# A convolution and mixture-of-experts kernel: the W stage's result kept as [output channel, w]

## The chip, the cores and the metric

The kernel runs on one core of one Trainium2 chip, in one launch. The metric is device microseconds for one execution. The names of the engines are those of the profile: PE is TensorE's matmul, PEld its load of the stationary operand, DVE VectorE, ACT ScalarE, POOL GpSimd, SP SyncE.

## The reference

Everything is fp32. Layer 0 is a convolution made of butterfly transforms along both image axes, added to its input after a group norm; layer 1 is an attention over the batch axis and a top-2 mixture of 8 experts, both on the tokens. Cut to what matters:

```python
# x: (32, 128, 64, 64); H = W = 64
def _kop2d(x, weight, kd1, kd2, k11, k12, k21, k22):
    xc, wc = x.astype(complex64), weight.astype(complex64)      # weight (128, 128, 3, 3)
    x_f = tensor_product(xc, _c(k11), _c(k12), False)           # butterflies along H, then along W
    w_f = tensor_product(wc, _c(kd1), _c(kd2), False) * math.sqrt(H * W)
    prod = jnp.einsum('bihw,oihw->bohw', x_f, w_f)
    return jnp.real(tensor_product(prod, _c(k21), _c(k22), True))

x = x + _kop2d(_gn(x), ...)                       # group norm over 32 groups of 4 channels
t = _to_tokens(x)                                 # (32, 4096, 128)
t = t + _L1_attn_ref(_ln_t(t), Wk, bk, Wv, bv)    # softmax((K^T V) / sqrt(32)) applied to the tokens
t = t + _L1_ffn_ref(_ln_t(t), ...)                # router, top 2 of 8 experts, weighted sum
x = _from_tokens(t, x)
```

## The kernel before

The butterflies are multiplied out at the start into dense matrices, and as the weight has only 3 x 3 taps the convolution becomes a sum over its rows p and columns q of three matrix products: over input channels, along w, along h. The 32 images are worked one after another, and each image's convolution runs in three rounds, one for each p. A round has three stages:

- `mix` (matmuls at L284): 16 groups g of two matmuls. The normalised image is the stationary operand, 128 pixels at a time, `wmix` (384 columns) the moving one. Four copies a group take the result out of PSUM into `y` [(q, w), channel, h].
- `along_w`, the W stage (matmuls at L304 and L312): 8 groups. The stationary operand is a contiguous piece of `y` with two channels, the moving one `ra` (128 columns) or `rb` (256). Each group fills two PSUM banks. Four copies a group take the result out into `u`, whose partitions are (real or imaginary, h). Each copy moves 64 partitions x 512 elements: 4 x 2 runs of 64 values of w, one run for each output channel.
- `along_h`, the H stage (matmuls at L334): 4 groups of 16 matmuls. Each takes all 128 output channels at one w from `u` as the stationary operand, and `lt[:, p, :]` with 64 columns as the moving one. DVE adds the group to the image (L338).

The trace holds two LDWEIGHTS and two MATMUL records for every `matmul` of the code: 64 matmuls of an H stage are 128 records.

The order is written by hand through generators: the H stage of a round is issued after the mix of the next round, so mix, H stage of the round before, W stage follow each other on TensorE, 96 times. All conv stages share two PSUM buffers of two banks (tag `cv`), and `y` and `u` are single buffers. An image's tail, which is the transposition to tokens, the attention and the experts (`tail`, L387 to L567), is cut into pieces, and a scheduler at the end of the kernel lays them between the pieces of the next image's convolution by estimated costs. The copies out of PSUM go through `evacuate`, which gives every fourth to DVE (L249) and the others to ACT (L251); copies of `y`, `u` and of the tail share this turn and these two lines. The program puts a wait between two copies of one group where one is on DVE and the other on ACT, so the four of a group run one after another.

On each engine instructions run in program order. An engine that waits for a copy holds up what is behind it.

## Time and profile before

| | |
|---|---|
| median of the runs | 12064.9 us (12059.3 to 12070.5, two runs) |
| profiled execution, span | 12065.3 us |
| PE busy | 10224.3 us, 85% |
| PEld busy | 7555.0 us, 63% |
| DVE busy | 6990.2 us, 58% |
| ACT busy | 6791.9 us, 56% |
| matmuls of the H stage (L334) | 12288 records, 1424.5 us busy |
| copies of u, ACT and DVE | 2304 and 768, 1036 and 1039 ns each |
| HBM traffic | 11 GB/s over the span |

Busy time is an average over stages that are held by different engines. The chain of waits says what set the end: it is followed back from the last instruction to what released it each time, and its shares are shares of the span. In the groups of instructions each line has engine, line of the kernel, operation, output and inputs, shapes and count; behind the first bar the busy time in all and the mean duration of one, behind the second the idle time before them and what ended most of it. TensorE's durations overlap in its pipe, so its pace is read from busy time and count, or from rows of consecutive matmuls. PEclk is the granted share of TensorE's clock.

### The profile page before, as it was taken

Reading aid. Unit: us, or ns where it says so; the run is one execution under the profiler, and the core shown is the slowest. Engines: PE = TensorE matmul, PEld = TensorE weight load, DVE = VectorE, ACT = ScalarE, POOL = GpSimd, SP = SyncE. Lnnn points to the kernel's source line nnn. Section 1 sums busy time; section 2 is a strip of 40 time slices with the busy share of each in tenths; the row PEclk is TensorE's granted clock in tenths of the full one; section 3 lists DMA queues with packets and bytes.
Section 4 is the critical chain, followed back from the end, with each engine's and each line's share of the span. In section 5 each row is a group of like instructions: output and inputs, shape, how many; then the busy total and the mean of one; then the engine's idle time right before and its main releaser. Section 6 shows DMA issues by size and latency. Waiting matters only on the chain.

```text
span 12065.3 us, 140418 instructions
## 1 busy us (share of the span) xinstructions
PE 10224.3 (85%) x53944; PEld 7555.0 (63%) x53944; DVE 6990.2 (58%) x17483; ACT 6791.9 (56%) x8609; POOL 694.6 (6%) x378
## 2 busy tenths in 40 slices
PE   6888888888888888888888888888888888888888
PEld 4666666666666566666666666665666666565665
DVE  4456655556555565555665555655556555566556
ACT  5655555565555655556555555556565555656552
POOL 0000000000000000000000000000000000000000
PEclk9999999999999999999999999999999999999998
DMA  0000000000000000000000000000000000000000
GB/s 27 9 13 8 15 12 13 12 15 8 13 12 13 14 8 13 13 13 13 8 14 12 13 13 12 11 12 13 12 15 8 13 12 13 14 8 14 12 6 13
DMA packets 44636, 146.90 MB, mean 12 GB/s; under 512 B 5186, under 2 KB 6596, under 8 KB 39876
## 3 DMA queue, kind: packets, MB, share of 16 engines
q1 hardware_dynamic: 42096, 137.19, 3.1%
q8 instruction: 432, 7.08, 0.2%
q14 instruction: 232, 1.90, 0.1%
q10 hardware_dynamic: 1876, 0.73, 0.0%
HBM read 70.79 MB, written 67.11 MB: 11 GB/s over the span
## 4 chain that ended last, share of the span: by engine, by line
PE 54%; ACT 31%; DVE 9%; issue 3%; POOL 3%; DMA 0%; POOLq 0%; ACTq 0%; DVEq 0%
ACT y L251 22%; PE ph L334 12%; PE pw L304 10%; PE pw L312 10%; PE pe L539 8%; DVE y L249 5%; PE pm L284 5%; ACT u L251 5%; POOL rs L383 3%; ACT at L462 3%; PE pl L488 3%; PE pg L414 2%; DVE u L249 1%; PE po L554 1%; PE po L555 1%
## 5 line engine op out<-in xcount | busy, mean ns | idle before, releaser
L251 ACT COPY u<-pw 64x512 f32<-64x512 f32 x2304 | 2386.4, 1036 | 3421.3 <-PE pw L312 2445.5
L251 ACT COPY y<-pm 64x384 f32<-64x384 f32 x4608 | 3728.4, 809 | 959.4 <-DVE y L249 526.6
L284 PE MATMUL pm<-wmix,xn 128*128 128x384 f32 x6144 | 2611.7, 550 | 1176.3 <-ACT y L251 708.9
L544 DVE SCALAR_TENSOR_TENSOR t<-pe,oh,t 128x128 f32<-128x128 f32 x8192 | 2771.4, 349 | 396.7 <-PE pe L539 108.1
L284 PEld LDWEIGHTS pm<-wmix,xn 128*128 128x128 f32 x6144 | 1137.2, 205 | 2437.7 <-ACT y L251 1310.1
L304 PEld LDWEIGHTS pw<-ra,y 128*128 128x128 f32 x12288 | 1845.6, 192 | 372.3 <-issue 185.1
L539 PE MATMUL pe<-ew_sb,xT 128*128 128x512 f32 x4096 | 1956.0, 595 | 44.2 <-DVE t L544 43.4
L249 DVE COPY y<-pm 64x384 f32<-64x384 f32 x1536 | 1234.6, 804 | 1234.3 <-ACT y L251 1033.0
L304 PE MATMUL pw<-ra,y 128*128 128x128 f32 x12288 | 1906.3, 277 | 10.1 <-DVE u L249 6.8
L312 PE MATMUL pw<-rb,y 128*128 128x256 f32 x6144 | 1853.7, 384 | 0.0
L334 PEld LDWEIGHTS ph<-lt,u 128*128 128x128 f32 x12288 | 1421.9, 195 | 128.7 <-ACT y L251 69.8
L249 DVE COPY u<-pw 64x512 f32<-64x512 f32 x768 | 797.6, 1039 | 1209.0 <-ACT u L251 1206.7
L334 PE MATMUL ph<-lt,u 128*128 128x64 f32 x12288 | 1424.5, 278 | 25.6 <-ACT y L251 17.2
L539 PEld LDWEIGHTS pe<-ew_sb,xT 128*128 128x128 f32 x4096 | 757.4, 190 | 676.3 <-issue 402.9
L312 PEld LDWEIGHTS pw<-rb,y 128*128 128x128 f32 x6144 | 941.1, 194 | 4.2 <-issue 0.5
L338 DVE TENSOR_TENSOR x<-ph,x 128x1024 f32<-128x1024 f32 x384 | 470.3, 1225 | 755.6 <-PE ph L334 754.7
L368 DVE BATCH_NORM_STATS2 bs<-t 128x6 f32<-128x128 f32 x2048 | 427.0, 279 | 468.8 <-POOL t L466 468.8
L383 POOL TENSOR_TENSOR rs<-m,mhalf 128x32 f32<-128x32 f32 x64 | 347.8, 5435 | 4528.2 <-DVE m L382 4528.2
L414 PE MATMUL pg<-xg 128*128 128x129 f32 x2048 | 295.0, 300 | 201.0 <-DVE xg L409 201.0
L483 PE MATMUL px<-ident,xn 128*128 128x128 f32 x1024 | 252.5, 371 | 206.1 <-DVE xn L479 206.1
L466 POOL TENSOR_TENSOR t<-t,at 128x512 f32<-128x512 f32 x256 | 324.5, 1267 | 1672.1 <-ACT at L462 1647.9
L414 PEld LDWEIGHTS pg<-xg 128*128 128x128 f32 x2048 | 283.2, 215 | 210.3 <-DVE xg L409 194.2
(132 smaller groups left out, 5560.8 us busy)
## 6 DMA issues: line engine op xcount, KB each, us to landing
x<-in_x_dram SPq DMA_DIRECT2D x32, 2048.0 KB
out_dram<-so SPq DMA_DIRECT2D x256, 256.0 KB
tws<-in_tw_dram SPq DMA_DIRECT2D x6, 384.0 KB
wmix<-in_conv_w_dram SPq DMA_DIRECT2D x1, 576.0 KB
ew_sb<-in_expert_w_dram ACTq DMA_DIRECT2D x1, 512.0 KB
eb_sb<-in_expert_b_dram ACTq DMA_DIRECT2D x16, 4.0 KB
wk_sb<-in_wkT_dram ACTq DMA_DIRECT2D x1, 64.0 KB
wv_sb<-in_wvT_dram ACTq DMA_DIRECT2D x1, 64.0 KB
```

Of the source, the lines that this page charges most:

```text
L249: nc.vector.tensor_copy(dst, src)
L251: nc.scalar.copy(dst, src)
L284: nc.tensor.matmul(ps[:, k, 0:384], xn[:, r : r + P], wmix[:, p, :], start=True, stop=True)
L304: nc.tensor.matmul(ps[:, bank, c0 + ab * P : c0 + (ab + 1) * P], yf[:, o * n : (o + 2) * n], ra, start=(k % 2 == 0 and ab == 0), stop=False,)
L312: nc.tensor.matmul(ps[:, bank, c0 : c0 + 256], yf[:, o * n : (o + 2) * n], rb.rearrange("w a m -> w (a m)"), start=False, stop=(k % 2 == 1),)
L334: nc.tensor.matmul(pf[:, k * n : (k + 1) * n], u[:, 16 * g + k, :], lt[:, p, :], start=True, stop=True)
L338: nc.vector.tensor_tensor(acc, pf.rearrange("o (w h) -> o h w", h=n), acc, ALU.add)
L368: nc.vector.bn_stats(bs[:, t].rearrange("p a s -> p (a s)"), src[:, t, :])
L383: nc.gpsimd.tensor_tensor(rstd, var, mhalf, ALU.pow)
L414: nc.tensor.matmul(pg[:, 0 : P + 1], xt[:, k, 0:P], xt[:, k, :], start=(i == 0), stop=(i == NT - 1))
L539: nc.tensor.matmul(ps, xT[:, i, :], ew_sb[:, 4 * half : 4 * half + 4, :].rearrange("d e c -> d (e c)"), start=True, stop=True,)
L544: nc.vector.scalar_tensor_tensor(t[:, i, :], ps[:, k * P : (k + 1) * P], gates[:, i, 4 * half + k : 4 * half + k + 1], t[:, i, :], ALU.mul ...
```

## The change

`u` is allocated as [partition, output channel, w] in place of [partition, w, output channel]. The copies of the W stage, which read the same 64-element runs of PSUM as before, then write each run to 64 consecutive elements, where they wrote elements 128 apart. The H stage's stationary operand, all output channels at one w, was 128 consecutive elements and is now 128 elements that lie 64 apart (256 bytes). Comments are also taken out of the file; they are left out of this diff.

```diff
     def along_w(b, p, y, u):
         yf = y.rearrange("w o h -> w (o h)")
-        uv = u.rearrange("h w (ab j r) -> h j ab r w", ab=2, r=2)
+        uv = u.rearrange("h (ab j r) w -> h j ab r w", ab=2, r=2)
...
     def along_h(b, p, u, xt):
...
                 nc.tensor.matmul(
-                    pf[:, k * n : (k + 1) * n], u[:, 16 * g + k, :], lt[:, p, :], start=True, stop=True
+                    pf[:, k * n : (k + 1) * n], u[:, :, 16 * g + k], lt[:, p, :], start=True, stop=True
                 )
...
     def conv():
...
-                u = yp.tile([P, n, P], F32, tag="u", name=f"u{b}_{p}")
+                u = yp.tile([P, P, n], F32, tag="u", name=f"u{b}_{p}")
```

## The prediction

> **What bounds the kernel now.** I read the page's first and fourth parts, then the groups with their shapes, then the chain of waits and the stretches around two H stages.

> ```profile
> span 12065.3 us, 140418 instructions
> PE 10224.3 (85%) x53944; PEld 7555.0 (63%) x53944; DVE 6990.2 (58%) x17483; ACT 6791.9 (56%) x8609; POOL 694.6 (6%) x378
> ...
> PE 54%; ACT 31%; DVE 9%; issue 3%; POOL 3%; DMA 0%; POOLq 0%; ACTq 0%; DVEq 0%
> ACT y L251 22%; PE ph L334 12%; PE pw L304 10%; PE pw L312 10%; PE pe L539 8%; DVE y L249 5%; PE pm L284 5%; ACT u L251 5%; POOL rs L383 3%; ACT at L462 3%; PE pl L488 3%; PE pg L414 2%; DVE u L249 1%; PE po L554 1%; PE po L555 1%
> ```

> TensorE holds over half of the chain. The mix stage (L284) is held by the copies of y, the W and H stages (L304, L312, L334) by TensorE. The two things that the change touches have very different weights there. The H stage's matmuls are 12% of 12065 us, 1448 us, and their whole busy time is 1424.5 us: practically every one of them is on the path. The copies of u are 5% on ACT and 1% on DVE, some 724 us, though ACT and DVE are busy with them for 3184 us.

> ```profile
> L251 ACT COPY u<-pw 64x512 f32<-64x512 f32 x2304 | 2386.4, 1036 | 3421.3 <-PE pw L312 2445.5
> L251 ACT COPY y<-pm 64x384 f32<-64x384 f32 x4608 | 3728.4, 809 | 959.4 <-DVE y L249 526.6
> L249 DVE COPY u<-pw 64x512 f32<-64x512 f32 x768 | 797.6, 1039 | 1209.0 <-ACT u L251 1206.7
> L334 PEld LDWEIGHTS ph<-lt,u 128*128 128x128 f32 x12288 | 1421.9, 195 | 128.7 <-ACT y L251 69.8
> L334 PE MATMUL ph<-lt,u 128*128 128x64 f32 x12288 | 1424.5, 278 | 25.6 <-ACT y L251 17.2
> ```

> The mean durations of 195 and 278 ns overlap in the pipe; the pace comes from busy time over count, 1424.5 us / 12288 = 116 ns, or from the chain, where 128 matmuls in a row take 14.40 us, 112 ns each.

> ```profile
> 3125.61 14.40 PE ph L334 x128
> 3140.01 0.50 PE pw L304 x4
> 3140.51 0.43 PE pw L312 x2
> 3140.94 0.44 PE pw L304 x4
> ```

> A matmul of 256 columns (L312) takes 0.43/2 = 0.215 us, one of 128 columns 0.44/4 = 0.11 us: 0.85 ns a column. Sixty-four columns therefore stream in 54 ns. The H stage runs at 112 ns, so it is not the streaming that paces it but the loading of 128 stationary columns, 0.87 ns each. A slower load has nothing to hide behind there.

> **The change, part by part.** The instructions of every engine, their order and their waits stay as they were; only the address patterns of the copies of u and of the 12288 stationary loads change.

> *The copies of u.* Their destination had consecutive elements 512 bytes apart; now they lie in runs of 64. For a contiguous copy of 512 elements the trace has rows:

> ```profile
> L251 ACT COPY so<-po 128x512 f32<-128x512 f32 x192 | 114.5, 597 | 109.3 <-PE po L555 106.3
> L249 DVE COPY xT<-px 128x512 f32<-128x512 f32 x64 | 44.3, 692 | 180.1 <-PE px L483 180.1
> ```

> So ACT's 1036 becomes about 600 ns (42% less) and DVE's 1039 about 690 (34% less). On the chain that is 0.42 x 603 + 0.34 x 121 = 294 us. This is the most that it can bring: copies off the chain are taken to give nothing. The least comes from the place where a copy must be on the path: the last group before the next mix, where four copies stand one behind another (chain at 3187.34, 1.03 + 1.03 + 1.05 + 1.06 us) with the first copy of y queued behind them on ACT. There the saving is 3 x 0.44 + 0.35 = 1.67 us, times 96 stages 160 us. Elsewhere the stall moves to TensorE: a group's matmuls, 16 records of 0.11 and 8 of 0.215 us, take 3.5 us, against 4.2 us of copies before and 2.5 after, so only part of the difference is won. I take 250 us.

> *The stationary load.* u is now read with neighbours 256 bytes apart. No load of before is strided, so the price has to be bounded. Below: nothing, the load keeps 112 ns. Above: by what writes of that stride cost. ACT's copies to y (stride 256 bytes) and to u (512 bytes) differ by 128 elements and 227 ns, 1.77 ns an element; DVE's, 804 and 1039 ns, by 1.84. Contiguous, ACT needs at most 597/512 = 1.17 ns an element with all its fixed cost. So both engines fall to one element in about 1.8 ns at either stride. Reads show the same trend:

> ```profile
> L375 DVE TENSOR_TENSOR m<-bs 128x32 f32<-128x32 f32 x64 | 13.8, 216 | 2.2
> L381 DVE TENSOR_TENSOR m<-m 128x32 f32<-128x32 f32 x64 | 11.8, 184 | 0.0
> ```

> L375 reads elements 24 bytes apart, L381 neighbours: 32 ns more for 32 elements, 1 ns each (L376, at 208, 0.75 ns). A load reads SBUF as these do, and its pace, 0.87 ns, is below 1.8 ns, so I take the strided pace: 128 x 1.77 = 227 ns in place of 112. Ends within this case: 208 ns (112 + 128 x 0.75) and 235 (128 x DVE's 1.84). The cost is 12288 x 115 ns = 1413 us; the ends are 1180 and 1511.

> [...]

> *The clock.* A slower H stage delivers fewer columns in a given time, and this trace shows what the granted clock makes of that:

> ```profile
> 276.44 25.17 PE ph L334 x128
> 301.60 0.96 PE pw L304 x4
> 302.56 0.85 PE pw L312 x2
> ```
> ```profile
> core 0: us, PE busy (x) PEld busy (x) DVE busy (x) ACT busy (x) POOL busy (x), PEclk, DMA share, GB/s
> 279.00:301.00 22.00, 22.00 (x106) 22.00 (x105) 5.12 (x5) 0.00 (x0) 0.00 (x0) 0.50 0.00 1
> 301.60:306.00 4.40, 4.40 (x18) 4.04 (x18) 1.22 (x1) 0.00 (x0) 0.00 (x0) 0.50 0.00 0
> 306.50:312.00 5.50, 4.75 (x32) 4.12 (x31) 1.02 (x1) 3.99 (x4) 0.00 (x0) 1.00 0.00 0
> ```

> This H stage fell to half clock and stayed there for 22 us while PE was busy in all of it. At half clock a contiguous load paces the stage at about 208 ns (22.00 us / 106), and 64 columns in 208 ns did not bring the clock back. A stage at 227 ns offers fewer still, so I expect most H stages to run at 0.50. That costs the loads nothing more if the pace of memory is the slower one (227 against 208), but the matmuls around pay: the W stage after it began at half clock for some 4.8 us and lost 2.4. I take 2 us x 96 = 192 (ends 0 and 230). One H stage in three has eight expert matmuls of 0.43 us between its own (1.72 us for four in the chain) and one has sixteen of 0.11: at half clock 5.2 us more an image, 166 us over 32; I take half, 83. It also means that a milder price for the stride is unlikely to stay mild: once the clock is halved the load needs 208 ns with or without a stride.

> [...]

> **Sum.** 12065 + 1413 + 192 + 83 - 250 = 13,503 us; I say 13,500. The profiled span, 12065.3, stands within half a microsecond of the median of 12064.9, so nothing is corrected. ACT and DVE have room during the longer H stage (in 14.40 us they were busy 2.65 and 8.11), but nothing that waits on TensorE later needs it.

> **Rivals.** *A strided load is free.* [...] Against it: two engines writing and one reading slow down. Then only the copies count: 12065 - 250 = 11,815 (11,771 to 11,905), faster or barely so. It holds as long as the load stays near 112 ns; from about +20 ns (250 us / 12288) the change no longer pays. Chance 0.15.
> *Stride and half clock add up.* If the line penalty of 115 ns comes on top of the halved pace, a load takes 208 + 115 = 323 ns: 12288 x 211 = 2593, and 12065 + 2593 + 275 - 250 = 14,683. For it: nothing says that the slower request rate absorbs the penalty. Against it: at half clock an element is asked for every 1.63 ns, close to what the strided writes reach anyway. Chance 0.09.
> *The clock holds.* Then 12065 + 1413 - 250 = 13,228, inside the forecast's own range. That the change does something else than it says has no ground: instructions and waits match one for one.

> **How the numbers follow.** Forecast 0.76, its own range 12,950 (1180 for the loads, no clock cost, 294 won) to 13,810 (1511 + 230 + 166 - 160). The range given, 12,900 to 14,700, takes in the adding-up rival and leaves out the free load and worse than 14,700, under 0.2 together. What a measurement of this kernel can tell from no change is about 2%, 241 us. Faster by more: most of the free-load case, 0.12. Within: the rest of it, 0.04. Slower: 0.84.

> **What would show it.** Right: the group L334 of PEld or PE with a busy time near 2800 us and 64 matmuls in a row near 14.5 us where they took 7.36; copies of u at 600 and 690 ns; granted clock 0.50 in H stages and half-clock starts of W; PE ph near 21% of the chain and ACT u near 3%. Wrong: H stages still at 14.40 us for 128 would make the free load true; 40 us or more for them the adding up. Copies of u still near 1030 ns would mean that their pace was not the stride's.

## The result, and the profile after

The changed kernel takes 13351.3 us (median of two runs, 13349.6 to 13353.0), against 12064.9 before: a ratio of 1.1062, with a 95% interval of 1.103 to 1.1094. It is slower by 1286 us. The forecast was 13,500 us, in a range of 12,900 to 14,700.

The page of the changed kernel, its engines and its chain:

```profile
span 13351.3 us, 140418 instructions
PE 11701.4 (88%) x53944; PEld 9011.7 (67%) x53944; DVE 6750.9 (51%) x17483; ACT 5735.3 (43%) x8609; POOL 694.6 (5%) x378
...
PE 64%; ACT 24%; DVE 7%; POOL 3%; issue 2%; DMA 0%; POOLq 0%; ACTq 0%; DVEq 0%
ACT y L251 20%; PE ph L334 20%; PE pw L304 10%; PE pw L312 10%; PE pe L539 10%; PE pm L284 5%; DVE y L249 5%; POOL rs L383 3%; ACT at L462 3%; PE pl L488 2%; PE pg L414 2%; PE po L554 1%; PE po L555 1%; PE px L483 1%; ACT u L251 1%
```

ACT and DVE have 1296 us less work together (1057 and 239) and the kernel is slower all the same. The H stage has gone from 12% to 20% of the chain; the copies of u have gone from 6% to 1%. The groups of the two parts (busy us, mean ns of one, idle before):

```profile
L334 PE MATMUL ph<-lt,u 128*128 128x64 f32 x12288 | 2707.2, 412 | 53.5 <-DVE y L249 34.7 <-ACT y L251 16.8
L334 PEld LDWEIGHTS ph<-lt,u 128*128 128x128 f32 x12288 | 2698.0, 311 | 187.7 <-issue 81.2 <-ACT y L251 69.4 <-DVE t L544 32.1
L251 ACT COPY u<-pw 64x512 f32<-64x512 f32 x2304 | 1334.5, 579 | 5418.7 <-PE pw L312 3938.5 <-DVE u L249 1464.7
L249 DVE COPY u<-pw 64x512 f32<-64x512 f32 x768 | 532.0, 693 | 673.2 <-ACT u L251 661.5 <-PE pw L312 2.8
```

The same instructions in the same order; the loads' busy time grew by 1276 us, and the copies of u fell from 1036 and 1039 ns to 579 and 693. The chain, and the granted clock in three stretches, around one H stage and the next:

```profile
3016.60 28.08 PE ph L334 x128
3044.68 0.96 PE pw L304 x4
3045.65 0.85 PE pw L312 x2
...
3141.51 14.20 PE ph L334 x64
3155.70 3.52 PE pe L539 x4
```
```profile
core 0: us, PE busy (x) PEld busy (x) DVE busy (x) ACT busy (x) POOL busy (x), PEclk, DMA share, GB/s
3016.60:3044.60 28.00, 28.00 (x129) 28.00 (x130) 8.81 (x16) 1.69 (x3) 0.00 (x0) 0.56 0.00 1
3044.70:3048.00 3.30, 3.30 (x15) 3.05 (x16) 3.28 (x9) 0.00 (x0) 0.00 (x0) 0.58 0.00 0
3049.00:3060.00 11.00, 11.00 (x47) 6.89 (x46) 8.26 (x27) 3.13 (x6) 0.00 (x0) 1.00 0.00 0
```

A load takes 28.08 us / 128 = 219 ns where it took 112. The granted clock is half in most of the stage (0.56 on average); the W stage behind it begins at half pace (0.85 us for two matmuls of 256 columns, before 0.43), and expert matmuls between those of the H stage take 3.52 us for four, before 1.77. Counted over all records, 74% of the H stage's matmuls start at half clock (before 2%), and the distance from one to the next is 218 ns at either clock.

### The profile page after: what moved, and what is told of

The parts are those of the page before. It is cut to its first block, busy times and chain, and to the rows that moved or that the text cites. A ratio compares the mean times of both kernels' runs of the same rounds, so it can differ in the third digit from the quotient of the medians.

```text
span 13351.3 us, 140418 instructions
## 1 busy us (share of the span) xinstructions
PE 11701.4 (88%) x53944; PEld 9011.7 (67%) x53944; DVE 6750.9 (51%) x17483; ACT 5735.3 (43%) x8609; POOL 694.6 (5%) x378
## 4 chain that ended last, share of the span: by engine, by line
PE 64%; ACT 24%; DVE 7%; POOL 3%; issue 2%; DMA 0%; POOLq 0%; ACTq 0%; DVEq 0%
ACT y L251 20%; PE ph L334 20%; PE pw L304 10%; PE pw L312 10%; PE pe L539 10%; PE pm L284 5%; DVE y L249 5%; POOL rs L383 3%; ACT at L462 3%; PE pl L488 2%; PE pg L414 2%; PE po L554 1%; PE po L555 1%; PE px L483 1%; ACT u L251 1%
## 5 line engine op out<-in xcount | busy, mean ns | idle before, releaser
L251 ACT COPY y<-pm 64x384 f32<-64x384 f32 x4608 | 3723.0, 808 | 914.5 <-DVE y L249 528.9
L251 ACT COPY u<-pw 64x512 f32<-64x512 f32 x2304 | 1334.5, 579 | 5418.7 <-PE pw L312 3938.5
L284 PE MATMUL pm<-wmix,xn 128*128 128x384 f32 x6144 | 2537.1, 537 | 1083.7 <-ACT y L251 645.2
L334 PEld LDWEIGHTS ph<-lt,u 128*128 128x128 f32 x12288 | 2698.0, 311 | 187.7 <-issue 81.2
L334 PE MATMUL ph<-lt,u 128*128 128x64 f32 x12288 | 2707.2, 412 | 53.5 <-DVE y L249 34.7
L284 PEld LDWEIGHTS pm<-wmix,xn 128*128 128x128 f32 x6144 | 1102.4, 199 | 2315.9 <-ACT y L251 1244.4
L304 PEld LDWEIGHTS pw<-ra,y 128*128 128x128 f32 x12288 | 1947.3, 202 | 370.3 <-issue 185.0
L539 PE MATMUL pe<-ew_sb,xT 128*128 128x512 f32 x4096 | 2061.0, 624 | 3.1 <-DVE t L544 2.3
L304 PE MATMUL pw<-ra,y 128*128 128x128 f32 x12288 | 1999.9, 287 | 3.3 <-DVE y L249 3.3
L312 PE MATMUL pw<-rb,y 128*128 128x256 f32 x6144 | 1921.4, 396 | 0.0
L249 DVE COPY y<-pm 64x384 f32<-64x384 f32 x1536 | 1235.9, 805 | 1206.6 <-ACT y L251 1009.2
L539 PEld LDWEIGHTS pe<-ew_sb,xT 128*128 128x128 f32 x4096 | 793.6, 199 | 660.0 <-issue 368.2
L312 PEld LDWEIGHTS pw<-rb,y 128*128 128x128 f32 x6144 | 986.0, 202 | 4.8 <-issue 1.0
L249 DVE COPY u<-pw 64x512 f32<-64x512 f32 x768 | 532.0, 693 | 673.2 <-ACT u L251 661.5
L383 POOL TENSOR_TENSOR rs<-m,mhalf 128x32 f32<-128x32 f32 x64 | 347.8, 5435 | 4978.1 <-DVE m L382 4978.1
L414 PE MATMUL pg<-xg 128*128 128x129 f32 x2048 | 294.6, 300 | 182.7 <-DVE xg L409 182.7
L483 PE MATMUL px<-ident,xn 128*128 128x128 f32 x1024 | 244.1, 359 | 226.8 <-DVE xn L479 226.8
L554 PE MATMUL po<-ident,t 128*128 128x128 f32 x2048 | 426.6, 293 | 1.8 <-DVE t L544 1.7
L483 PEld LDWEIGHTS px<-ident,xn 128*128 128x128 f32 x1024 | 183.7, 187 | 350.6 <-DVE xn L479 236.4
```

The costliest lines, as they stand in the source:

```text
L249: nc.vector.tensor_copy(dst, src)
L251: nc.scalar.copy(dst, src)
L284: nc.tensor.matmul(ps[:, k, 0:384], xn[:, r : r + P], wmix[:, p, :], start=True, stop=True)
L304: nc.tensor.matmul(ps[:, bank, c0 + ab * P : c0 + (ab + 1) * P], yf[:, o * n : (o + 2) * n], ra, start=(k % 2 == 0 and ab == 0), stop=False,)
L312: nc.tensor.matmul(ps[:, bank, c0 : c0 + 256], yf[:, o * n : (o + 2) * n], rb.rearrange("w a m -> w (a m)"), start=False, stop=(k % 2 == 1),)
L334: nc.tensor.matmul(pf[:, k * n : (k + 1) * n], u[:, :, 16 * g + k], lt[:, p, :], start=True, stop=True)
```

## The experiments

The theory: a strided load takes 218 ns where a contiguous one takes 112, 106 ns longer; beside the slower H stage the clock falls to half, which costs more in the stages around; the copies give some of it back. Each of these has a run of its own.

**The copies alone.** The H stage takes contiguous elements (others than it should).

```diff
-  u[:, :, 16 * g + k]
+  u.rearrange("h o w -> h (o w)")[:, (16 * g + k) * P : (16 * g + k + 1) * P]
```

> The new copies alone: u is written in runs of 64 as in the changed kernel, but the H stage takes 128 consecutive elements as its stationary operand (so it multiplies other elements of u than it should; amounts of work, order and waits are the same). Theory (strided loads cost 106 ns each, copies save on their own): L334 back to 14.4 us for 128 in a row at clock 1.0, copies of u 579 and 693 ns as in the changed kernel, time 11,770 to 11,905 us, best guess 11,815. Rival (the copies bring nothing of their own, since TensorE holds the W stage): 12,065 us within 0.5%. Rival (the H stage is slow for another reason than the stride of the load, such as the place of u): H stage stays at 28 us for 128.

Measured: 11941 us, ratio 0.9885 (0.9859 to 0.9911): a gain of 128 us, and 36 us above the expected range. The copies take 579 and 693 ns, as in the changed kernel. What the theory had missed stands in this kernel's chain and windows:

```profile
3086.81 2.76 PE pm L284 x4
3089.57 27.20 PE ph L334 x128
3116.77 0.96 PE pw L304 x4
```
```profile
3089.60:3116.80 27.20, 27.20 (x129) 27.20 (x129) 8.06 (x15) 2.62 (x4) 0.00 (x0) 0.50 0.00 1
3117.00:3121.00 4.00, 4.00 (x23) 3.72 (x23) 3.55 (x10) 0.00 (x0) 0.00 (x0) 0.73 0.00 0
```

With contiguous loads 14 of the 96 H stages run at half clock: one of them falls to it 2.7 us after its start, like the one in the kernel before that the prediction showed, and 13 begin at half clock and stay there to their end, which none does in the kernel before. Such a stage takes 27.20 us in place of 14.4. Ahead of these 13 stages run the router's matmuls (L488, 8 columns), and among them the clock goes to half (in the kernel before it is 0.85 from 3109.0 to 3113.5 us and 0.50 from 3113.7 to 3118.5); four mix matmuls at 2.76 us, before the H stage, are still slow; and in these H stages, with 64 columns every 213 ns, the clock stays at 0.50.

From the first matmul of an H stage to that of the W stage, the H stages take 1913 us together, against 1753 before. The profiled execution is 115 us shorter than before's; without the 160 the copies would have gained 275.

**The load alone.** The copies of before, and a strided load from that layout (other elements than it should).

```diff
-  u[:, 16 * g + k, :]
+  u.rearrange("h w o -> h (w o)").rearrange("h (a c) -> h a c", c=n)[:, :, 16 * g + k]
```

> The strided load alone: u is written as in the kernel before (elements 512 bytes apart), and the H stage takes 128 elements that lie 256 bytes apart (other elements than it should; same amounts, order and waits). Theory: 218 ns a load, half clock in most of the H stage, copies of u at 1036 and 1039 ns: the changed kernel without its saving, 13,351 + 250 = 13,600 us (13,510 to 13,650). If the two parts are independent, e1 and e2 add up: e1 + e2 - before = changed kernel, within 50 us. Rival (the longer H stage hides the copies' cost, so the copies' part is smaller here): 13,351 to 13,450 us.

Measured: 13683 us, ratio 1.1339 (1.1322 to 1.1356), 33 us above the expected range. Its loads and its copies on ACT:

```profile
L334 PEld LDWEIGHTS ph<-lt,u 128*128 128x128 f32 x12288 | 2698.4, 311 | 136.6 <-ACT y L251 69.3 <-DVE t L544 25.8 <-issue 25.7
L251 ACT COPY u<-pw 64x512 f32<-64x512 f32 x2304 | 2384.4, 1035 | 4736.3 <-PE pw L312 3214.2 <-DVE u L249 1501.5
```

The load alone costs 1615 us against before's 12068.7 in these rounds, and the copies are worth 13683 - 13351 = 332 us beside it. The parts don't add up: 11941 + 13683 - 12069 = 13,555, 204 us more than the changed kernel, and not within the 50 us that were expected. By the stages of the profiled executions (table in the next section) the gap, 215 us there, is 134 in the H stages and 81 in the W stages, none in the mix stages. The first is the copies' run, whose H stages lost 160 us to the clock; beside slow loads the H stages are mostly at half clock anyway (74% of the records in the changed kernel), and there is little left to lose. The second is what the copies save more in the W stage beside slow loads.

**The clock.** The changed kernel, with 128 moving columns for 14 of 16 matmuls; the next one overwrites the second half. `lt` gets a fourth, zeroed entry, so that the wider piece exists for the last p.

```diff
-  lt = cp.tile([P, 3, n], F32, name="lt")
+  lt = cp.tile([P, 4, n], F32, name="lt")
+  nc.gpsimd.memset(lt, 0.0)
...
+  wide = int(k % 8 != 7)
-  pf[:, k * n : (k + 1) * n], u[:, :, 16 * g + k], lt[:, p, :]
+  pf[:, k * n : (k + 1 + wide) * n], u[:, :, 16 * g + k], lt[:, p : p + 1 + wide, :].rearrange("h a m -> h (a m)")
```

> The changed kernel with more columns streamed for each load: 14 of 16 matmuls of an H group take 128 moving columns in place of 64; the next matmul overwrites the second half, so the output is the same. A matmul of 128 columns streams 107 ns, still less than a load's 218. Theory (half clock comes from too few columns in a window, and costs on the path): clock 1.0 in the H stages, mean clock above 0.94 in place of 0.859, loads still 218 ns, H stage still 28 us for 128 in a row, expert matmuls between them and the start of the W stage at full pace; time 13,351 less 200 to 350, best guess 13,080 us. [...] Rival (the clock comes back but nothing on the path needs it): clock above 0.94, time 13,351 within 0.5%.

Measured: 13056 us, ratio 1.082 (1.0804 to 1.0836), 295 us faster than the changed kernel. The chain and the windows of an H stage and the W stage after it:

```profile
280.98 28.31 PE ph L336 x128
```
```profile
281.00:309.00 28.00, 28.00 (x128) 28.00 (x128) 7.50 (x8) 1.58 (x2) 0.00 (x0) 1.00 0.00 1
309.40:314.00 4.60, 4.60 (x34) 4.34 (x33) 1.15 (x1) 1.09 (x2) 0.00 (x0) 1.00 0.00 0
```

The stage takes as long as in the changed kernel, 28.31 us against 28.08, so the strided load's price is the same at either clock here; but the clock is 1.00 where it was 0.56, and W begins at full pace. PE was busy throughout in both, 28.00 of 28.00 us. What differs is the number of columns streamed for each load, 128 against 64, so the clock goes with the columns here; halved, it costs 295 us on the path.

**What makes a stride dear.** Three runs with the stationary elements 8, 12 and 16 bytes apart (others than it should take), everything else as in the changed kernel.

```diff
-  u[:, :, 16 * g + k]
+  u.rearrange("h o w -> h (o w)")[:, bass.ds((16 * g + k) % (n - 1) * P, P, step=2)]
```

(This is the step of 2 elements; those of 3 and 4 have n - 2 and n - 3.)

> The changed kernel, with the H stage's 128 stationary elements taken 8 bytes apart (other elements than it should; copies as in the changed kernel). [...] Rival (any step other than one halves the pace): 218 ns a load, time 13,350 us.

> The same with elements 12 bytes apart. [...] Rival (a cliff at a step over 8 bytes): 218 ns at full clock, time 13,350. Rival (a cliff at 16 bytes): 112 ns, 11,890 to 11,960.

> [...] Rival (the price grows with the distance, so 256 bytes is dear and 16 cheap): under 180 ns, time under 13,000.

One run each: 11961, 13131 and 13572 us. The first is at the upper end of the 11,890 to 11,960 that stood for a load of 112 ns, the second between that and the 13,350 that stood for 218 ns, the third 1.7% above 13,350. Rows of consecutive H matmuls from the three chains, in this order:

```profile
5312.52 15.47 PE ph L334 x128
```
```profile
4329.17 5.43 PE ph L334 x32
```
```profile
186.88 30.13 PE ph L334 x128
```

These are 121, 170 and 235 ns each; the median distances from one record to the next at full clock are 118, 173 and 233 ns. The price is nearly absent at 8 bytes, 118 ns against 112 for a contiguous load, and fully there at 16 bytes, 233 ns; 12 bytes lie between, 173 ns. So "any step other than one" doesn't fit, as 8 bytes cost 6 ns; a single cliff, below 12 bytes or above, doesn't, as 173 is neither 112 nor 218; and "the farther the dearer" doesn't, as 16 bytes apart cost 233 ns and 256 bytes 218. What makes the price come in between 8 and 16 bytes is not shown by these runs, and why 16 bytes are dearer than 256 is open.

In these three runs 9%, 65% and 79% of the H stage's matmuls start at half clock. The prediction's remark that a milder price would not stay mild holds for 173 ns a load, and not for 118.

**Both sides fast.** The output channels are relabelled in the arranged weight so that the eight channels of one copy of u are neighbours; u is again [w, channel], copies write runs of 32 bytes and read PSUM with a large inner step, and loads are contiguous.

```diff
-  uv = u.rearrange("h w (ab j r) -> h j ab r w", ab=2, r=2)
+  uv = u.rearrange("h w (g r a j) -> h g r w a j", r=2, a=2, j=4)
...
-  uv[c * n : (c + 1) * n, 4 * g : 4 * g + 4, :, r, :], pv[...]
+  uv[c * n : (c + 1) * n, g, r], pv[...].rearrange("m j a w -> m w a j")
...
+  pos = np.arange(128).reshape(8, 2, 2, 4).transpose(2, 0, 3, 1).reshape(-1)
+  w = w[..., pos]
```

> Both sides at once: the output channels are relabelled in the arranged weight, so that the eight channels of one copy of u are neighbours; u stays [w, channel], a copy writes runs of 8 elements (32 bytes, runs 512 bytes apart) and reads PSUM with inner strides of 512 and 1024 bytes; the H stage's load is contiguous. [...] Rival (only a long contiguous run is fast): copies 800 to 1040 ns, time 11,950 to 12,065. Rival (PSUM reads slow down where the inner step is large): copies over 1040 ns, time 12,065 or more.

Measured: 11924 us, ratio 0.9881 (0.9844 to 0.9918), runs from 11873 to 11976; the median is 19 us above the 11,770 to 11,905 us that were expected here as for the copies alone. The copies take 579 and 693 ns, exactly as with runs of 64. It loses to the clock in the same way as the copies alone: 11 H stages at half clock in the profiled run, like the one of its chain shown here below its copies on ACT:

```profile
L251 ACT COPY u<-pw 64x512 f32<-64x512 f32 x2304 | 1334.3, 579 | 4191.7 <-PE pw L312 3300.0 <-DVE u L249 876.1
```
```profile
864.80 27.20 PE ph L334 x128
```

**And the clock kept up**, with the same wide moving operand as above:

> The version with relabelled channels (short runs on the writing side, contiguous loads), and 128 moving columns for 14 of 16 matmuls of the H stage, overwritten by the next one. Theory (the copies save 280 us or more, and in the two versions with contiguous loads some 100 to 180 of it went to H stages that start at half clock and with 64 columns a load can't get out of it): H stages at clock 1.0, 14.0 to 14.5 us for 128 in a row everywhere, mean clock above 0.95; time 11,925 less 110 to 200, best guess 11,770 us, and the runs as close together as before's (within 30 us). Rival (128 columns in 107 ns beside a load of 112 slow the H stage, or the clock has another cause): 11,900 us or more.

Measured: 11733 us (11727 to 11740), ratio 0.9714 (0.9698 to 0.973) against before's 12081 in these rounds, and 191 us below the version without it. The spread of the runs fell from 104 to 13 us. The number of H stages at half clock can be counted in the profiled run alone, but the mean granted clock says the same of the others: the four runs without the wide operand took 11873, 11898, 11949 and 11976 us at 0.939, 0.937, 0.932 and 0.929. The first H stages of its chain, and the group:

```profile
186.72 14.51 PE ph L336 x128
268.91 14.51 PE ph L336 x128
```
```profile
L336 PE MATMUL ph<-lt,u 128*128 128x128 f32 (+1 forms) x12288 | 1407.8, 275 | 50.9 <-DVE y L250 31.7 <-ACT y L252 17.2
```

No H stage stays at half clock here, and streaming twice the columns costs the stage nothing (14.51 us against 14.40), as the load paced it (54 ns of streaming in 112).

**Neighbours at the dearer copies.** The copies of y are also strided: each writes two rows in turn, with the elements of a row 256 bytes apart, and takes 809 ns on ACT and 804 on DVE for 384 elements. The group norm now writes rows in another order, so that a copy writes pairs of neighbours.

```diff
-  nc.vector.tensor_scalar(xn[:, sl], xt[:, sl], ...)
+  for o in range(2):
+      nc.vector.tensor_scalar(xn[:, sl].rearrange("c (g k o w) -> c g k o w", ...)[:, :, :, o],
+                              xt[:, sl].rearrange("c (g o k w) -> c g o k w", ...)[:, :, o], ...)
...
-  y[half * n : (half + 1) * n, :, bass.ds(4 * g + odd, 2, step=2)].rearrange("w o k -> w k o"), ps[...]
+  y[half * n : (half + 1) * n, :, 4 * g + 2 * odd : 4 * g + 2 * odd + 2], ps[...].rearrange("w k o -> w o k")
```

> The last version, and the same rule applied to the copies of y: the group norm writes the image's rows in another order, so that the two rows of one copy are neighbours in y and a copy writes pairs of elements (8 bytes, pairs 256 bytes apart), reading the two banks of PSUM in turn. [...] Rival (alternating between PSUM banks slows the read): copies at 800 ns or more, time 11,733 or more.

Measured: 10634.9 us, ratio 0.8808 (0.8792 to 0.8824), the fastest of all. The groups of the copies and the chain:

```profile
L252 ACT COPY y<-pm 64x384 f32<-64x384 f32 x4608 | 2237.2, 486 | 1207.0 <-PE pm L290 614.2 <-DVE y L250 534.6
L250 DVE COPY y<-pm 64x384 f32<-64x384 f32 x1536 | 850.6, 554 | 471.9 <-ACT y L252 330.2 <-PE pm L290 100.7
...
PE 70%; issue 12%; DVE 8%; ACT 5%; POOL 5%; DMA 0%; POOLq 0%; DVEq 0%; SPq 0%; ACTq 0%
PE pe L546 14%; PE pm L290 14%; PE ph L341 13%; PE pw L310 10%; PE pw L318 10%; ACT y L252 4%; POOL rs L390 3%; PE pl L495 3%; DVE y L250 3%; PE po L561 2%; PE po L562 2%; DVE bs L375 2%; DVE t L551 2%; POOL t L473 1%; PE px L490 1%
```

A copy of y takes 486 and 554 ns in place of 809 and 804. ACT's copies of y were 22 to 24% of the chain and are 4%; the mix matmuls went from 5% to 14%. The kernel gains 1098 us against the version above, and by the traces 1088 of them lie in the mix stages. The change that this document is about lost 1286, as it made the loads strided to make the copies contiguous. "issue" has grown to 12% of the chain, time in which the engine waited for nothing that the profile shows; no run says what stands behind it.

## Why the prediction was right, and where it was off

TensorE's time by stage, in us, added up from the traces: from the first matmul of a stage to the first of the next one, over all 96 rounds, pieces of the tail included.

| | mix | H | W |
|---|---|---|---|
| before | 5486.7 | 1753.0 | 4754.4 |
| the copies alone | 5369.2 | 1913.3 | 4595.5 |
| the load alone | 5482.0 | 3161.0 | 4966.6 |
| the changed kernel | 5365.5 | 3186.9 | 4726.4 |
| the changed kernel with wide matmuls | 5358.6 | 3098.6 | 4523.3 |

- **The weights on the path.** The H stage was taken to be wholly on the path, the copies by their share of the chain. Both held in direction: the loads' busy time grew by 1276 us, the H stages by 1434, the mix and W stages fell by 121 and 28, and the kernel grew by 1286.
- **The load.** Predicted 227 ns, by the slope of ACT's strided copies; measured 219 in the chain, 218 between records. The term was 12288 x 115 = 1413 us and is 12288 x 106 = 1303: 110 too large, and between the ends given. That a load pays for such a stride what a copy pays was an assumption; 218/128 = 1.70 ns an element against the copies' 1.77 shows it for this one.
- **The clock.** Predicted 275 us, from one H stage that had fallen to half clock before; 295 measured, by the run with the wide matmuls. By stage it is 203 us in W and 88 in H, where 192 and 83 were taken, so the two places were right as well as the sum. Both figures had been chosen between wide ends, and that they came so close is in part luck. That the load itself doesn't pay for it was right too: 218 ns at either clock, which ends the rival of stride and half clock adding up. The "line penalty" that this rival adds is shown by no run as such; the runs show that a stride of 256 bytes makes a load 106 ns longer than a contiguous one at full clock (218 against 112) and 5 at half clock (218 against 213). The 208 ns for a contiguous load at half clock is 213 by the distances between records.
- **The copies.** Predicted 250 us, at least 160 and at most 294. Beside contiguous loads they save 118 us in the mix stages and 159 in the W stages, some 276 and within these bounds. Beside slow loads they are worth 332, above the bound: 116 in mix and 240 in W, and the H stages take 26 more. This step failed at its upper bound: "copies off the chain are taken to give nothing". It has no term for what shorter copies do to the clock. By the records, a W stage spends 6.9 us at half clock in the load's own run and 5.5 in the changed kernel; half of the difference times 96 is 64 us, which would leave 268. That part is worked out, not shown by a run. The chain's share of ACT's copies fell to 1%, not to the 3% named as a sign.
- **The sum.** 1303 + 295 - 332 = 1266, against 1286 measured. The sum of 13,503 was high by 152: 110 from the load, 82 from the copies, and the other way 20 from the clock and 20 that stay unexplained. The terms are not quite separate, as the copies' 332 hold some of the clock.
- **The free-load rival** was not only wrong on the load. Its own time, 11,815 us, was too low: the two runs with contiguous copies and contiguous loads took 11,941 and 11,924, as H stages at half clock took most of the gain, in the first 160 of 275 us. A contiguous H stage stuck at half clock stands in the prediction itself, but was counted only as a price of slow loads. With shorter copies the H stages begin at other times: for those that begin at half clock, the next point of the clock's grid came within 0.8 us in the kernel before and comes up to 2.6 us later with the copies alone.

## What to carry to other kernels

Before a layout is turned to make one side contiguous, ask who reads it, and which of the two is on the path: here 3072 copies, mostly hidden, were traded against 12288 loads that were all on it. Here there was a third layout: runs of 8 elements on the writing side left the loads contiguous, because labels of channels or rows can be permuted where the data is arranged or normalised anyway. Two fp32 elements side by side, or 8 bytes apart, came close to full pace here: 118 ns against 112 for a load of elements 8 bytes apart, and 486 ns against 809 for a copy of y in pairs. Where loads pace TensorE and few columns stream behind each, look at the granted clock, and stream more columns if there is room: here 128 columns in place of 64 took an H stage from 0.56 to 1.00.

## What the hardware showed that was not expected

- The pace of a contiguous copy needs no long run: runs of 8 elements cost the same 579 ns as runs of 64, and pairs of elements 486 ns for 384, while PSUM was read with inner steps of 1 KB or from two banks in turn.
- A stage with 64 columns to each contiguous load ran at either clock: 112 ns a matmul at 1.00 and 213 at 0.50. What went with the one and the other can be counted. Take the intervals of the grid of 3.41 us on which the clock changes, and count the columns streamed in each as a share of what full clock could stream (an expert matmul's 512 take 0.43 us). In the trace of before the clock fell after 131 intervals, all with a share of at most 0.36, and stayed at 1.00 after 2976, all with at least 0.37; at half clock it came back after 131, with at least 0.38, and stayed after 272, with at most 0.35. In that of the changed kernel it fell after 317, with at most 0.38, stayed at 1.00 after 2467, with at least 0.37, came back after 317, with at least 0.37, and stayed at half after 785, with at most 0.38. An H stage of before has 54 ns of streaming in 112, a share of 0.48, and 65 of the 96 ran wholly at 1.00; in 213 or 218 ns the share is 0.25, and the stages above stayed at 0.50 with it; 128 columns in 218 ns make 0.49, and the clock there was 1.00. So it is likely, by these counts, that the interval at the start of a stage, which it shares with what ran ahead, chooses between the two; no run varied that interval alone. The runs of one kernel that spread by 104 us differ in their granted clock, 0.939 to 0.929, as this would have it.
- Elements 16 bytes apart load slower (233 ns) than elements 256 bytes apart (218 ns).
